# Two graph layers on one core: block sums of the last batch made earlier, the last graph's tail in another order

## The chip, the cores and the metric

One core of a Trainium2 chip. The metric is the device time of one launch in microseconds (us). A profile covers one execution; times without a profile come from further executions on the same chip. Runs e1 to e8 were made on one chip, e9 and e10 on another, each set beside its own nine runs of the kernel before. Medians are given with their number of runs. All timed runs of this study were in the fast state; the runs that were looked at once are of state "unknown", as for any single run on fewer than eight cores, and their mean granted clock (0.996 to 0.998) is that of the fast runs.

## The reference, cut to what matters

64 graphs of 256 nodes with 256 channels go through two layers. The first makes messages between nodes, a convolution along the nodes and the gates of a recurrent cell; the second aggregates over the adjacency. After each layer the result is added to its input and normed.

```python
# layer 0, per graph (n = 256 nodes, d = 256)
x_in = concatenate([x_conv, x_nmp])              # convolution, messages
gi, gh = x_in @ w_ih.T + b_ih, x @ w_hh.T + b_hh
r, z = sigmoid(gi_r + gh_r), sigmoid(gi_z + gh_z)
x = layernorm(x + (1 - z) * tanh(gi_n + r * gh_n) + z * x)
# layer 1
h = layer_norm(x)
agg = einsum('bij,bjh->bih', adj, h)
x = layernorm(x + relu(agg @ W_rel + b_rel + h @ W_root))
```

## The kernel before

The convolution is done for eight graphs (a batch) at a time. It is spread over the graphs of the batch ahead of it: `pump()` lets it go on a little after each piece of a graph. In the traces of this case each engine's operations stand in the order in which the program issues them (VectorE's gn at 2241.99 stayed behind an h that waited for GpSimd, although its input was ready at 2240.24), so the order of the calls below is read as the order on every engine.

The last batch (graphs 56 to 63) has no convolution to hide, and its graphs 56 to 62 compute the gates by a block scheme with seven products in the place of eight. These need sums of blocks of the three inputs (xT, the graph's nodes transposed; nmp, the messages; xc, the convolution), which VectorE makes. Code is cut here and below; `...` marks what is left out:

```python
    def block_sums(k, i):                 # i: 0 = xT, 1 = nmp, 2 = xc
        ...
        nc.vector.tensor_add(s1, a21, a22)
        nc.vector.tensor_sub(s2, s1, a11)
        nc.vector.tensor_sub(s3, a11, a21)
        nc.vector.tensor_sub(s4, a12, s2)
        LEFT[k, i] = (a11, a12, s4, a22, s1, s2, s3)

    def block_gates(k):
        ...
        a, d = bank("ps_a"), bank("ps_d")          # no sums needed
        onto(0, 0, product(a, 0, True), 0)
        onto(0, 0, product(d, 1, True))
        yield
        b_, c_ = bank("ps_b"), bank("ps_c")        # sums of all three inputs
        onto(1, 1, product(b_, 4, True), 1)
        onto(1, 1, product(c_, 6, True))
        yield
        ...

    # between the batches
        for _ in coming:
            pass
    ...
    first_k = (NB - 1) * BG               # graph 56
    for i in range(3):
        block_sums(first_k, i)
    for k in range(first_k, B - 1):
        ...                               # block_gates(k), update(k), second layer of k - 1
    last_graph(y_left, B - 1)
```

The last graph (63) is computed in two halves of 128 nodes, so that its chain (gates, norm, transposes, projection, aggregation, norm, store) can overlap with itself:

```python
        def half(n):
            ...                                    # nn: two operations on VectorE, then
            nc.scalar.activation(a, a, AF.Tanh)
            yield
            ...                                    # w: three operations, statistics on VectorE
            q = scales(mv, [...])                  # root, on GpSimd
            nc.vector.tensor_scalar(H[k][:, n, :], c, mv[:, 0:1], q[:, 1:2], ALU.subtract, ALU.mult)
            sh = shift(mv, q)                      # two GpSimd instructions
            yield
            nc.scalar.activation(X1[k][:, n, :], c, AF.Identity, bias=sh, scale=q[:, 0:1])
            yield
        ...
        gates_n(k, 1)
        step(halves_[1])
        turn_half(0)
        project(k - 1)
        project_half(0)
        step(halves_[1])
        turn_half(1)
        agg = aggregate(k - 1)
        step(agg)
        project_half(1)
        ...
```

Of the kernel before, what the change touches and what calls it, by code (L numbers as in the profile page):

```python
# [29 lines left out]
BG = 8  # L30
# [46 lines left out]
def gnn_two_layers(  # L77
# [357 lines left out]
    def conv(b):  # L435
# [122 lines left out]
        def third(j):  # L558
            stt(sl(V + j, 2, 8), sl(V + j, 2, 8), sv[j], sl(U + j, 2, 8))
            yield cost(2)  # L560
# [25 lines left out]
            yield from second(j)  # L586
        for j in range(8):
            yield from third(j)

        def channels(q):  # L590
            for o in range(C):
# [165 lines left out]
    def block_sums(k, i):  # L757

        if i == 2:
            xc, g = XC[k]  # L760
            v = xc[:, :, g, :]
        else:
            v = (XT, NMP)[i][k]
        a11, a12, a21, a22 = (v[:, c, n * P:(n + 1) * P] for n in range(C) for c in range(C))
        at = S * D + ((k % 2) * 3 + i) * 4 * P
        s1, s2, s3, s4 = (XF[:, at + j * P:at + (j + 1) * P] for j in range(4))
# [5 lines that stand above are left out]
# [102 lines left out]
    def project(k):  # L874
        hT = H[k]
        hr = work.tile([P, C, D], F32, tag="hr", name="hr", bufs=1)
        outs = []
        for n in range(C):
            ps = bank("ps_out")
            for c in range(C):  # L880
                nc.tensor.matmul(ps, hT[:, c, n * P:(n + 1) * P], wrr[:, c, :], start=(c == 0), stop=(c == C - 1))  # L881
            nc.scalar.copy(hr[:, n, :], ps[:, :D])  # L882
            outs.append(ps)
        OUTS[k] = (hr, outs)
# [29 lines left out]
    def step(g):  # L914
        if g is not None:
            next(g, None)


    def last_graph(y_before, k):
        nn, w, y = (work.tile([P, C, D], F32, tag=t, name=t, bufs=b) for t, b in (("nn", 1), ("w", 1), ("y", 2)))  # L920
        H[k] = work.tile([P, C, D], F32, tag="h", name="h", bufs=1)
        X1[k] = work.tile([P, C, D], F32, tag="x1", name="x1", bufs=2)

        hT, hr = (XF[:, i * C * D:(i + 1) * C * D].rearrange("p (c n) -> p c n", c=C) for i in range(2))
        outs = []

        def scales(mv, columns):

            q = work.tile([P, 2], F32, tag="q", name="qh", bufs=4)
            for i, (f, e) in enumerate(columns):  # L930
                nc.gpsimd.tensor_scalar(q[:, i:i + 1], mv[:, 1:2], f, e, ALU.mult, ALU.add)
            nc.gpsimd.tensor_tensor(q[:, :len(columns)], q[:, :len(columns)], mhalf[:, :len(columns)], ALU.pow)
            return q

        def shift(mv, q):
            sh = work.tile([P, 1], F32, tag="sh", name="shh", bufs=4)
            nc.gpsimd.tensor_mul(sh, mv[:, 0:1], q[:, 0:1])
            nc.gpsimd.tensor_scalar(sh, sh, -1.0, None, ALU.mult)
            return sh

        def half(n):
            rz, gn = RZ[k]
            a, c = nn[:, n, :], w[:, n, :]
            stt(a, rz[:, n, :D], 1.0, gn[:, n, D:], op0=ALU.add, op1=ALU.mult)
            stt(a, a, 0.5, gn[:, n, :D])
            nc.scalar.activation(a, a, AF.Tanh)
            yield
            nc.vector.tensor_sub(c, XG[k][:, n, :], a)
            stt(c, rz[:, n, D:], 3.0, c, op0=ALU.add, op1=ALU.mult)
            stt(c, a, 4.0, c)  # L950
            mv = work.tile([P, 1, 2], F32, tag="mv", name="mvh", bufs=4)
            stats(mv, 0, c)
            mv = mv[:, 0, :]
            q = scales(mv, [(1.0, 4 * EPS), (1 + EPS, 4 * EPS * EPS)])
            nc.vector.tensor_scalar(H[k][:, n, :], c, mv[:, 0:1], q[:, 1:2], ALU.subtract, ALU.mult)
            sh = shift(mv, q)
            yield
            nc.scalar.activation(X1[k][:, n, :], c, AF.Identity, bias=sh, scale=q[:, 0:1])
            yield

        def turn_half(n):
            ps = bank("ps_hT")
            for c in range(C):
                nc.tensor.transpose(ps[:, c * P:(c + 1) * P], H[k][:, n, c * P:(c + 1) * P], ident)
            for c in range(C):
                nc.scalar.activation(hT[:, c, n * P:(n + 1) * P], ps[:, c * P:(c + 1) * P], AF.Identity,
                                     bias=gb[:, 1, c:c + 1], scale=gb[:, 0, c:c + 1])

        def project_half(n):
            ps = bank("ps_out")  # L970
            for c in range(C):
                nc.tensor.matmul(ps, hT[:, c, n * P:(n + 1) * P], wrr[:, c, :], start=(c == 0), stop=(c == C - 1))
            nc.scalar.copy(hr[:, n, :], ps[:, :D])
            outs.append(ps)

        halves_ = [half(n) for n in range(C)]
        gates_rz(k, 0)
        gates_n(k, 0)
        step(y_before)
        transposes_h(k - 1)  # L980
        step(halves_[0])
        gates_rz(k, 1)
        step(halves_[0])
        step(halves_[0])
        gates_n(k, 1)
        step(halves_[1])
        turn_half(0)
        project(k - 1)
        project_half(0)
        step(halves_[1])  # L990
        turn_half(1)
        agg = aggregate(k - 1)
        step(agg)
        project_half(1)
        step(halves_[1])
        step(agg)
        for m in range(C):
            for n in range(C):
                nc.tensor.matmul(outs[n][:, D:], ADJ[k][:, m, n * P:(n + 1) * P], hr[:, m, :], start=False,
                                 stop=(m == C - 1), skip_group_check=True)  # L1000
        step(agg)
        for n in range(C):
            o = y[:, n, :]
            nc.vector.tensor_add(o, outs[n][:, D:], brel)
            stt(o, o, 0.0, X1[k][:, n, :], op0=ALU.max, op1=ALU.add)
            mv = work.tile([P, 1, 2], F32, tag="mv3", name="mvy", bufs=4)
            stats(mv, 0, o)
            q = scales(mv[:, 0, :], [(1.0, EPS / 4)])
            sh = shift(mv[:, 0, :], q)
            nc.scalar.activation(o, o, AF.Identity, bias=sh, scale=q[:, 0:1])  # L1010
            (nc.sync, nc.scalar)[n].dma_start(out=out[k, n * P:(n + 1) * P, :], in_=o)


# [108 lines left out]
    POINTS = 10  # L1122
    y_left = None
    sums_left = weight_blocks()
    for b in range(NB):
        coming = conv(b + 1) if b + 1 < NB else iter(())
        done, at, goal = 0.0, 0, BG * POINTS - 6

        def pump():
            nonlocal done, at  # L1130
            at += 1
            while done < CONV_WEIGHT * at / goal:
                t = next(coming, 1e9)
                if t is None:
                    break
                done += t
            if STAGE.get(NB - 1) == "inverse":
                next(sums_left, None)

        if b == NB - 1:  # L1140
            break
        for k in range(b * BG, min((b + 1) * BG, B - 1)):
            load(k + 3)
            load_x(k + 1)
            up = update(k)
            agg = None
            gates_rz(k, 0)
            pump()
            gates_n(k, 0)
            step(y_left)  # L1150
            pump()
            if k > 0:
                transposes_h(k - 1)
            pump()
            gates_rz(k, 1)
            pump()
            if k + 1 < B:
                passing(k + 1)
            pump()
            if k + 2 < B:  # L1160
                factors(k + 2)
            gates_n(k, 1)
            pump()
            if k > 0:
                project(k - 1)
            step(up)
            pump()
            if k + 2 < B:
                distances(k + 2)
            step(up)  # L1170
            pump()
            if k + 3 < B:
                messages(k + 3)
            step(up)
            pump()
            if k + 2 < B:
                mask(k + 2)
            if k > 0:
# [3 lines that stand above are left out]
            pump()  # L1182
            y_left = agg
        for _ in coming:
            pass
    for _ in sums_left:
        pass
    first_k = (NB - 1) * BG
    for i in range(3):
        block_sums(first_k, i)  # L1190
    for k in range(first_k, B - 1):
        load(k + 3)
# [74 lines left out]
```

## Time and profile before

| | before |
|---|---|
| median of 3 runs | 2264.42 us (2263.78 to 2267.38) |
| span of the profiled run | 2261.8 us |
| TensorE busy | 2211.9 us (98%) |
| VectorE busy | 1720.1 us (76%) |

The page, the waits and the timelines that matter are shown in the prediction below. To compare many runs, I cut each trace at four points, and use two stretches throughout:

- the **transition**: from the first matmul of graph 56's ps_a to the ps_hT that follows it. Both kernels have the same twelve fp32 matmuls in it, which the trace shows as twenty-four rows (x2 for each);
- the **tail**: from the first matmul of ps_rz of graph 63 to the issue of the last store.

The two starts in the kernel before, from TensorE's timeline. A row has the start and the duration in us, the engine (PE is TensorE, DVE VectorE, ACT ScalarE, POOL GpSimd, ACTq ScalarE's queue of transfers), the line of the program, the operation, what it writes <- what it reads, the shapes and the number of instructions merged; a bracket gives the idle time of the engine just before it and what ended that:

```profile
2054.70 0.59 PE L785 MATMUL ps_a<-whh,xT 128*128 128x256 f32 x2
...
2224.15 1.88 PE L712 MATMUL ps_rz<-whh,xT 128*128 128x512 f32 x4
```

With ps_hT at 2066.78 the transition is 2066.78 - 2054.70 = 12.08 us, and with the last store at 2258.93 the tail is 34.78 us.

### The profile page before, as it was taken

Reading aid. Unit: us, or ns where it says so; the run is one execution under the profiler, and the core shown is the slowest. Engines: PE = TensorE matmul, PEld = TensorE weight load, DVE = VectorE, ACT = ScalarE, POOL = GpSimd, SP = SyncE. Lnnn points to the kernel's source line nnn. Section 1 sums busy time; section 2 is a strip of 40 time slices with the busy share of each in tenths; the row PEclk is TensorE's granted clock in tenths of the full one; section 3 lists DMA queues with packets and bytes.
Section 4 is the critical chain, followed back from the end, with each engine's and each line's share of the span. In section 5 each row is a group of like instructions: output and inputs, shape, how many; then the busy total and the mean of one; then the engine's idle time right before and its main releaser. Section 6 shows DMA issues by size and latency. Waiting matters only on the chain.

```text
span 2261.8 us, 24648 instructions
## 1 busy us (share of the span) xinstructions
PE 2211.9 (98%) x8400; PEld 1463.5 (65%) x8400; DVE 1720.1 (76%) x3328; ACT 767.7 (34%) x1588; POOL 469.9 (21%) x935
## 2 busy tenths in 40 slices
PE   8999999999999999999999999999999999999998
PEld 5775666666665666656666666665666666666664
DVE  6966889388883988749886497956889388896675
ACT  6433223532234322443224432253223432233333
POOL 0101212221220221213112121221212221222122
PEclk9999999999999999999999999999999999999999
DMA  5932433214423153232522243232432314421110
GB/s 148 316 112 65 139 103 98 98 43 140 135 75 103 38 166 104 79 103 79 163 68 83 91 129 127 70 98 67 138 107 90 100 48 140 135 75 38 42 33 19
DMA packets 212682, 226.69 MB, mean 100 GB/s; under 512 B 22103, under 2 KB 203854, under 8 KB 212558
## 3 DMA queue, kind: packets, MB, share of 16 engines
q1 hardware_dynamic: 190128, 191.27, 26.8%
q10 hardware_dynamic: 22430, 33.86, 4.3%
q8 instruction: 67, 1.10, 0.2%
q14 instruction: 57, 0.47, 0.1%
HBM read 179.22 MB, written 45.88 MB: 100 GB/s over the span
## 4 chain that ended last, share of the span: by engine, by line
PE 79%; DVE 16%; issue 2%; POOL 1%; ACT 1%; DMA 1%; ACTq 0%; POOLq 0%; DVEq 0%
PE ps_rz L714 15%; PE ps_k L385 10%; PE ps_rz L712 8%; PE ps_n L726 7%; PE ps_out L881 7%; DVE XF L104 5%; PE ps_c L466 5%; PE ps_nmp L696 5%; PE ps_msg L646 4%; PE ps_out L893 4%; PE ps_n L724 4%; PE ps_w L230 2%; DVE w L104 2%; DVE bst L823 1%; PE ps_xc L594 1%
## 5 line engine op out<-in xcount | busy, mean ns | idle before, releaser
L104 DVE SCALAR_TENSOR_TENSOR XF<-XF 128x512 f32<-128x512 f32 (+2 forms) x800 | 507.3, 664 | 7.4
L845 POOL TENSOR_SCALAR q<-mv 128x2 f32<-128x2 f32 x63 | 31.8, 506 | 1448.8 <-DVE mv L824 1448.8
L385 PE MATMUL ps_k<-w,XF 128*128 128x256 f32 x1316 | 300.6, 384 | 14.7 <-ACT AT L686 11.6
L385 PEld LDWEIGHTS ps_k<-w,XF 128*128 128x128 f32 x1316 | 247.5, 191 | 62.7 <-ACT AT L686 17.2
L727 DVE TENSOR_TENSOR gn<-ps_n,brzn 128x512 f32<-128x512 f32 x114 | 78.1, 685 | 199.9 <-PE ps_n L726 199.9
L718 ACT ACTIVATE rz<-rz 128x512 f32<-128x512 f32 x114 | 71.8, 630 | 461.4 <-DVE rz L717 461.4
L881 PE MATMUL ps_out<-wrr,hT 128*128 128x512 f32 x504 | 226.6, 592 | 0.0
L712 PE MATMUL ps_rz<-whh,xT 128*128 128x512 f32 x456 | 215.5, 595 | 0.0
L714 PE MATMUL ps_rz<-wih,xc 128*128 128x512 f32 x456 | 214.3, 592 | 0.0
L714 PE MATMUL ps_rz<-wih,nmp 128*128 128x512 f32 x456 | 214.3, 592 | 0.0
L717 DVE TENSOR_TENSOR rz<-ps_rz,brzn 128x512 f32<-128x512 f32 x114 | 77.5, 680 | 155.0 <-PE ps_rz L714 155.0
L881 PEld LDWEIGHTS ps_out<-wrr,hT 128*128 128x128 f32 x504 | 95.7, 190 | 96.1 <-issue 84.2
L714 PEld LDWEIGHTS ps_rz<-wih,xc 128*128 128x128 f32 x456 | 86.7, 190 | 109.0 <-issue 108.8
L714 PEld LDWEIGHTS ps_rz<-wih,nmp 128*128 128x128 f32 x456 | 86.7, 190 | 109.0 <-issue 109.0
L657 ACT ACTIVATE msg<-msg 128x512 f32<-128x512 f32 x61 | 38.4, 630 | 338.8 <-DVE msg L655 338.8
L646 PE MATMUL ps_msg<-wms,xT 128*128 128x260 f32 x512 | 131.9, 395 | 4.6 <-DVE XF L401 4.6
L362 DVE TENSOR_TENSOR XF<-XF 128x512 f32<-128x512 f32 (+3 forms) x128 | 126.1, 1010 | 1.7
L466 PE MATMUL ps_c<-xTc,w 128*128 128x512 f32 x256 | 116.1, 596 | 6.9 <-ACT xTc L458 6.9
L696 PE MATMUL ps_nmp<-AT,msg 128*128 128x256 f32 x512 | 121.1, 379 | 0.0
L712 PEld LDWEIGHTS ps_rz<-whh,xT 128*128 128x128 f32 x456 | 82.7, 192 | 58.3 <-issue 55.1
L882 ACT COPY hr<-ps_out 128x256 f32<-128x256 f32 x126 | 46.8, 372 | 214.7 <-PE ps_out L881 214.7
L893 PE MATMUL ps_out<-hr,adj 128*128 128x256 f32 x504 | 119.5, 380 | 0.0
(196 smaller groups left out, 3787.8 us busy)
## 6 DMA issues: line engine op xcount, KB each, us to landing
w<-w2m SPq DMA_DIRECT2D x105, 768.0 KB, 5.9
xn<-in_x_dram SPq DMA_DIRECT2D x32, 512.0 KB, 4.4
xt<-xTc ACTq DMA_DIRECT2D x32, 512.0 KB, 3.3
xT<-xt SPq DMA_DIRECT2D x64, 256.0 KB, 3.0
xb<-in_x_dram SPq DMA_DIRECT2D x32, 512.0 KB, 5.9
adj<-in_adjT_dram SPq DMA_DIRECT2D x64, 256.0 KB, 2.8
x<-in_x_dram SPq DMA_DIRECT2D x64, 256.0 KB, 3.0
out_dram<-y ACTq DMA_DIRECT2D x63, 256.0 KB, 2.2
```

What stands on the lines that cost most here:

```text
L104: nc.vector.scalar_tensor_tensor(o, in0, s, in1, op0=op0, op1=op1)
L362: (nc.vector.tensor_add if add else nc.vector.tensor_sub)(sl(o, n), sl(a, n), sl(b, n))
L385: nc.tensor.matmul(ps, X[:, slot, c * P:(c + 1) * P], w(m, c), start=(c == 0), stop=(c == C - 1))
L466: nc.tensor.matmul(pss[o], w1[:, c, o * P:(o + 1) * P], xTc[:, c, :], start=(c == 0), stop=(c == C - 1))
L646: nc.tensor.matmul(ps[:, :D + 4], XT[k][:, c, m * P:(m + 1) * P], wms[:, c, :], start=(c == 0), stop=(c == C - 1 and not idle))
L696: nc.tensor.matmul(ps[:, d * N:(d + 1) * N], MSG[k][:, m, d * P:(d + 1) * P], AT[k][:, m, :], start=(m == 0), stop=(m == C - 1))
L712: nc.tensor.matmul(prz, XT[k][:, c, q], whh[:, c, 0:2 * D], start=(c == 0), stop=False)
L714: nc.tensor.matmul(prz, t, wih[:, i, 0:2 * D], start=False, stop=(i == 3))
L724: nc.tensor.matmul(pn[:, D:], XT[k][:, c, q], whh[:, c, 2 * D:], start=(c == 0), stop=(c == C - 1))
L726: nc.tensor.matmul(pn[:, :D], t, wih[:, i, 2 * D:], start=(i == 0), stop=(i == 3))
L881: nc.tensor.matmul(ps, hT[:, c, n * P:(n + 1) * P], wrr[:, c, :], start=(c == 0), stop=(c == C - 1))
L893: nc.tensor.matmul(po, ADJ[k][:, m, n * P:(n + 1) * P], hr[:, m, :], start=False, stop=(m == C - 1), skip_group_check=True)
```

## The change

Its intent: take TensorE's wait for the sums away by making them where VectorE idles, in the batch before; let the second half of the last graph start on VectorE before the first half's root is back from GpSimd, with TensorE's order to match; and let VectorE apply the last norm, so that two GpSimd instructions and one of ScalarE fall off the end. In `pump()` one set of sums goes out per call, once the last batch's convolution is in its output stage and graph 56's messages are there; the condition on `done` keeps the last set, that of xc, until that convolution has run out.

```diff
@@ conv(b)
         for j in range(8):
             yield from third(j)
+        STAGE[b] = "out"
@@ half(n)
             q = scales(mv, [(1.0, 4 * EPS), (1 + EPS, 4 * EPS * EPS)])
+            yield
             nc.vector.tensor_scalar(H[k][:, n, :], c, mv[:, 0:1], q[:, 1:2], ALU.subtract, ALU.mult)
@@ last_graph
         step(halves_[0])
-        step(halves_[0])
         gates_n(k, 1)
         step(halves_[1])
+        step(halves_[0])
+        step(halves_[0])
+        project(k - 1)
+        step(halves_[1])
         turn_half(0)
-        project(k - 1)
-        project_half(0)
         step(halves_[1])
-        turn_half(1)
         agg = aggregate(k - 1)
         step(agg)
+        turn_half(1)
+        step(halves_[1])
+        project_half(0)
         project_half(1)
-        step(halves_[1])
         step(agg)
@@ last_graph, last norm
-            sh = shift(mv[:, 0, :], q)
-            nc.scalar.activation(o, o, AF.Identity, bias=sh, scale=q[:, 0:1])
+            if n == 0:
+                sh = shift(mv[:, 0, :], q)
+                nc.scalar.activation(o, o, AF.Identity, bias=sh, scale=q[:, 0:1])
+            else:
+                nc.vector.tensor_scalar(o, o, mv[:, 0, 0:1], q[:, 0:1], ALU.subtract, ALU.mult)
@@ main loop
+    early_sums = [0, 1, 2]
@@ pump()
-            if STAGE.get(NB - 1) == "inverse":
+            if STAGE.get(NB - 1) in ("inverse", "out"):
                 next(sums_left, None)
+            if STAGE.get(NB - 1) == "out" and (NB - 1) * BG in NMP and len(early_sums) > (done < 1e8):
+                block_sums((NB - 1) * BG, early_sums.pop(0))
@@ behind the batches
-    for i in range(3):
+    for i in early_sums:
         block_sums(first_k, i)
```

## The prediction

> **What bounds the kernel now.** I read the page first. TensorE is the bound from end to end:
>
> ```profile
> PE 2211.9 (98%) x8400; PEld 1463.5 (65%) x8400; DVE 1720.1 (76%) x3328; ACT 767.7 (34%) x1588; POOL 469.9 (21%) x935
> ```
>
> Of a span of 2261.8 us TensorE is idle for 2261.8 - 2211.9 = 49.9 us, so no change that leaves its work alone can win more than 2.2%. This change adds or removes no matmul. It works on two places only, so the next view is what TensorE waited for in the last 262 us (engine, line, releaser; then total us, times, longest):
>
> ```profile
> PE ps_b L785 <- DVE XF L767: 2.7, 2, 2.5
> PE ps_hT L964 <- DVE h L955: 2.3, 2, 2.0
> ```
>
> The first wait is where the last batch's first graph (56) starts: its blocked products need sums of blocks that VectorE makes. The second is in the last graph. The timeline of TensorE at the first place (start us, us, then the instructions merged), with graph 57 below for comparison:
>
> ```profile
> 2060.83 0.67 PE L785 MATMUL ps_b<-wsum,XF 128*128 128x256 f32 x2 [2.52 <-DVE XF L767]
> 2061.69 2.27 PE L785 MATMUL ps_b<-wsum,XF 128*128 128x384 f32 x4 [0.19 <-DVE XF L767]
> 2063.76 3.19 PE L785 MATMUL ps_c<-wsum,XF 128*128 128x256 f32 x6
> 2066.78 0.60 PE L868 MATMUL ps_hT<-ident,h 128*128 128x128 f32 x4
> ...
> 2087.25 1.89 PE L785 MATMUL ps_b<-wsum,XF 128*128 128x256 f32 x6
> ...
> 2090.69 0.60 PE L868 MATMUL ps_hT<-ident,h 128*128 128x128 f32 x4
> ```
>
> The matmuls ahead of ps_b started at 2057.50 and streamed until 2058.14 (as the same pair in graph 57: 2086.60 to 2087.25). From there to ps_hT graph 56 takes 2066.78 - 2058.14 = 8.64 us, graph 57 takes 2090.69 - 2087.25 = 3.44 us for the same twelve instructions. The excess is 5.20 us: more than the 2.7 us of waits in the list. The windows tell why (columns: stretch, length, busy PE, PEld, DVE, ACT, POOL, then the granted clock, DMA share, GB/s):
>
> ```profile
> 2060.80:2063.70 2.90, 2.66 (x6) 1.22 (x7) 2.83 (x12) 1.09 (x2) 1.40 (x4) 0.87 0.00 0
> 2063.70:2066.70 3.00, 3.00 (x7) 1.80 (x6) 1.09 (x3) 0.00 (x0) 0.00 (x0) 0.55 0.26 87
> ```
>
> After the hole the clock falls to about half for some 3.6 us. Now VectorE's timeline before that hole, to see whether the sums could be made sooner:
>
> ```profile
> 2041.75 0.69 DVE L717 TENSOR_TENSOR rz<-ps_rz,brzn 128x512 f32<-128x512 f32 x1 [3.99 <-PE ps_rz L714]
> 2047.16 0.69 DVE L727 TENSOR_TENSOR gn<-ps_n,brzn 128x512 f32<-128x512 f32 x1 [4.72 <-PE ps_n L726]
> ...
> 2051.53 0.69 DVE L836 TENSOR_TENSOR w<-x,nn 128x512 f32<-128x512 f32 x1 [2.15 <-ACT nn L832]
> ...
> 2060.43 0.26 DVE L767 TENSOR_TENSOR XF<-xT 128x128 f32<-128x128 f32 x1
> ```
>
> The bracket is the idle time ahead of a row. VectorE stood idle for 3.99, 4.72 and 2.15 us, and made the sums only at 2060.43, last in its queue. Finally the tail, all engines:
>
> ```profile
> 2241.67 0.41 DVE L955 TENSOR_SCALAR h<-w,mvh,qh 128x256 f32<-128x256 f32 x1 [1.36 <-POOL qh L932]
> ...
> 2241.99 0.68 DVE L727 TENSOR_TENSOR gn<-ps_n,brzn 128x512 f32<-128x512 f32 x1
> ...
> 2242.23 0.41 PE L964 MATMUL ps_hT<-ident,h 128*128 128x128 f32 x2 [1.99 <-DVE h L955]
> ...
> 2247.54 0.41 DVE L955 TENSOR_SCALAR h<-w,mvh,qh 128x256 f32<-128x256 f32 x1 [1.37 <-POOL qh L932]
> ...
> 2257.10 0.58 POOL L932 TENSOR_TENSOR qh<-qh,mhalf 128x1 f32<-128x1 f32 x1
> 2257.38 0.36 SPq L1011 DMA_DIRECT2D out_dram<-y  x1
> ...
> 2258.30 0.60 ACT L1010 ACTIVATE y<-y,shh,qh 128x256 f32<-128x256 f32 x1 [0.94 <-POOL shh L938]
> 2258.93 0.35 ACTq L1011 DMA_DIRECT2D out_dram<-y  x1
> ```
>
> VectorE's queue is in order: h of the first half waits 1.36 us for GpSimd's root, and gn of the second half stands behind it although its PSUM was ready at 2240.24. The end hangs on that second half: gn 2241.99, h 2247.54, then matmuls, two norms, and the store issued at 2258.93.
>
> [...] the trace's sums took 0.26 to 0.30 us, and 2.78 us for all twelve from start to start (2060.43 to 2063.21). [...] I use the starts of what follows a GpSimd instruction.
>
> **Part 1, the block sums.** The built order of VectorE shows twelve additions moved: the four of xT go behind the second rz of graph 55, the four of nmp behind its gn, the four of xc behind its two nn. Nothing is added. Costs: 4 x 0.23 = 0.93 us each. The xT sums fall into 4.72 us of idle (2042.4 to 2047.16): free. The nmp sums (copy of nmp done at 2046.4, in time) push nn from 2047.96 to about 2048.8, its end to about 2050.3; ScalarE's tanh of nn stands behind the copy of hr that starts at 2050.60 anyway, so nothing is later. The xc sums take 2050.3 to 2051.2, ahead of w at 2051.53: free.
> TensorE then runs on: ps_b at 2058.14, ps_c at 2059.86, ps_hT at 2061.58. What might bind next: h for ps_hT (done 2057.30), and VectorE's read of ps_a, which now follows the statistics of y at 2060.43 and ends at about 2061.0, against 2062.0 where TensorE needs it. So the whole 8.64 - 3.44 = 5.20 us goes: about 2.9 us of waiting for sums, the rest the slow clock and smaller waits behind it. From 2067 to 2209 TensorE has no gap in this trace, so the gain is carried to the end: -5.2 us.
>
> **Part 2, the order of the last graph.** h of the first half moves behind nn of the second. Then gn starts when ps_n is there and the statistics are done, about 2240.32 instead of 2241.99. From gn to h of the second half the old trace has 2247.54 - 2241.99 = 5.55 us; the first h (0.41) drops into the 0.48 us that VectorE waits for tanh there, cost about 0.05. So h starts at 2240.32 + 5.55 + 0.05 = 2245.92, 1.62 sooner. TensorE meanwhile does project of graph 62 (2240.08 to 2243.52), one pair of transposes and the aggregation to about 2245.5, then idles about 1 us for h. Behind h, old and new have 0.24 us of transposes and then 3.44 us of matmul before the last aggregation (old: adjacency and half a projection; new: two half projections), and the hr copy bounds the last aggregation alike. So the aggregation and all behind it come 1.62 us sooner, even though project_half(0) now stands behind the idle time.
>
> **Part 3, last norm on VectorE.** Old: from the end of the root (2257.69) two GpSimd instructions and ScalarE, DMA issued at 2258.93: 1.24 us. New: one VectorE operation of 0.41 us, like h, which starts 0.03 us behind the root (2241.64 to 2241.67), and 0.07 us to the queue: 0.51. Gain 0.73 us. The two stores of 128 KB now start 0.82 instead of 1.55 us apart and may share the engines: +0.1.
> Sum, all estimates from these rows: -5.2 - 1.62 - 0.73 + 0.1 = -7.4 us; 2264.42 - 7.4 = 2257.0 us, 0.33%.
>
> **Rivals.** (a) The moved sums delay graph 55: if idle time were not there, up to 2.8 us would come back in w and its norm. For: nmp does push nn by 0.9. Against: the three idle times above. It would leave 2259.8. (b) The clock drop is not the hole's doing[...] and only the waits go: 2.9 instead of 5.2, time 2259.3. Against: the granted clock reads 1.00 in every stretch I sampled around it. (c) In the tail the idle 1 us before the second transposes, or the projection placed behind it, eats the 1.62: then 2258.6; and if the clock dropped there, about 2 us more. Against: the old tail's hole of 1.99 us left the clock at 1.00. (d) TensorE binds on VectorE's read of ps_a sooner than I put it: up to 0.9 us, as before graph 62's ps_a at 2209.97.
>
> **Range and chances.** The three runs of before spread over 3.6 us, half of the effect, so the range is the rivals (up to +2.5) and that spread: 2254.5 to 2260.5. The verdict line of 2% is 45 us away; TensorE's idle time altogether is 50 us, and slower by 45 us would need a loss in a part that is not touched. Within 2%: 0.98, faster 0.01, slower 0.01.
>
> **What would show it.** Right: no wait of ps_b for the sums; graph 56's ps_b to ps_hT in 3.4 us at clock 1.00; ps_hT of graph 55 near 2061.6; the second h of the tail about 5.6 us behind its gn and 6.8 us sooner in absolute time; no GpSimd shift before the last store, whose issue lies about 7.5 us sooner, at 2251.4; span near 2254.3. Wrong: nn, w or y of graph 55 later than before, a clock below 0.9 anywhere behind 2055, a hole before the second transposes above 1.5 us, or last rows that are sooner by less than 5 us.

## The result, and the profile after

| | before | changed | ratio of fast runs, 95% interval |
|---|---|---|---|
| first timing | 2265.89 us (4 runs) | 2255.80 us (4 runs, 2254.62 to 2256.83) | 0.9956 [0.9939, 0.9973] |
| timed again | 2261.97 us (9 runs, 2259.09 to 2265.19) | 2254.73 us (5 runs, 2252.30 to 2256.18) | 0.9968 [0.9956, 0.9981] |

A ratio is the mean time of one kernel's fast runs over that of the other's fast runs of the same rounds, so it is not quite the ratio of the medians. Both timings are "same" by the 2% rule, and both are clearly faster. The first says 10 us and the second 7.2; the prediction said 7.4. What is known of the difference stands under e9.

The profiled run of the changed kernel has a span of 2252.8 us, 9.0 less. TensorE's waits from 2000 us on (total, times, longest) no longer name the sums, and the wait for h in the tail is down from 1.99 at its longest to 0.6:

```profile
PE ps_a L786 <- DVE XF L791: 0.9, 1, 0.9
PE ps_dist L685 <- ACT lr L676: 0.7, 1, 0.7
PE ps_hT L966 <- DVE h L957: 0.6, 1, 0.6
```

TensorE's timeline of the transition, and the start of the tail:

```profile
2053.25 0.60 PE L786 MATMUL ps_a<-whh,xT 128*128 128x256 f32 x2
...
2056.69 1.89 PE L786 MATMUL ps_b<-wsum,XF 128*128 128x256 f32 x6
2058.41 1.89 PE L786 MATMUL ps_c<-wsum,XF 128*128 128x256 f32 x6
2060.13 0.60 PE L869 MATMUL ps_hT<-ident,h 128*128 128x128 f32 x4
...
2217.52 1.88 PE L713 MATMUL ps_rz<-whh,xT 128*128 128x512 f32 x4
```

No bracket, so no idle time: ps_b to ps_hT takes 3.44 us where it took 5.95 from ps_b's late start and 8.64 from the end of ps_d. The transition is 6.88 us, 5.20 less. The granted clock in that stretch (columns as in the prediction: stretch, length, busy times of five engines, clock, DMA share, GB/s) is full, where it had been 0.55 and 0.87:

```profile
2056.70:2060.20 3.50, 3.50 (x14) 2.29 (x13) 3.26 (x10) 0.10 (x1) 2.00 (x5) 1.00 0.00 0
```

VectorE's timeline shows where the sums went. The last row's bracket is the idle time that is left ahead of w, which has not moved against TensorE (w is 3.18 us ahead of ps_a's first matmul, as it was 3.17 before):

```profile
2040.90 0.28 DVE L768 TENSOR_TENSOR XF<-xT 128x128 f32<-128x128 f32 x1
...
2046.32 0.28 DVE L768 TENSOR_TENSOR XF<-nmp 128x128 f32<-128x128 f32 x1
...
2048.57 0.29 DVE L768 TENSOR_TENSOR XF<-xc 128x128 f32<-128x128 f32 x1
...
2050.07 0.69 DVE L837 TENSOR_TENSOR w<-x,nn 128x512 f32<-128x512 f32 x1 [0.49 <-ACT nn L833]
```

The tail, all engines:

```profile
2233.64 0.69 DVE L728 TENSOR_TENSOR gn<-ps_n,brzn 128x512 f32<-128x512 f32 x1
...
2239.19 0.41 DVE L957 TENSOR_SCALAR h<-w,mvh,qh 128x256 f32<-128x256 f32 x1 [1.37 <-POOL qh L933]
...
2239.66 0.44 PE L966 MATMUL ps_hT<-ident,h 128*128 128x128 f32 x2 [0.61 <-DVE h L957]
...
2247.14 0.85 POOL L933 TENSOR_TENSOR qh<-qh,mhalf 128x1 f32<-128x1 f32 x1
...
2248.65 0.19 POOL L932 TENSOR_SCALAR qh<-mvy 128x1 f32<-128x1 f32 x1
2248.92 0.58 POOL L933 TENSOR_TENSOR qh<-qh,mhalf 128x1 f32<-128x1 f32 x1
...
2249.54 0.41 DVE L1017 TENSOR_SCALAR y<-y,mvy,qh 128x256 f32<-128x256 f32 x1 [1.29 <-POOL qh L933]
2249.98 0.35 ACTq L1018 DMA_DIRECT2D out_dram<-y  x1
```

From gn to the second h it is 5.55 us, as before; gn itself comes sooner. The tail is 2249.98 - 2217.52 = 32.46 us, 2.31 less. One thing is new: VectorE's statistics of the second half are done at 2248.24, but the second root begins at 2248.65, because GpSimd is still busy with the first half.

So the profile's 9.0 us are 5.20 in the transition, 2.31 in the tail, and 1.45 ahead of graph 56 (its ps_a starts at 2053.25 instead of 2054.70), where the two programs are the same until the sums at 2040.90. That last part lies within the scatter of this stretch, which the next section shows.

### The profile page after: what moved, and what is told of

It reads as the page before. It is cut to its first block, busy times and chain, and to the rows that moved or that the text cites. A ratio compares the mean times of both kernels' runs of the same rounds, so it can differ in the third digit from the quotient of the medians.

```text
span 2252.8 us, 24641 instructions
## 1 busy us (share of the span) xinstructions
PE 2210.0 (98%) x8400; PEld 1465.9 (65%) x8400; DVE 1721.0 (76%) x3329; ACT 767.1 (34%) x1587; POOL 469.8 (21%) x933
## 4 chain that ended last, share of the span: by engine, by line
PE 80%; DVE 15%; issue 2%; POOL 1%; ACT 1%; DMA 1%; ACTq 0%; SPq 0%; POOLq 0%; DVEq 0%
PE ps_rz L715 15%; PE ps_k L385 11%; PE ps_rz L713 8%; PE ps_n L727 7%; PE ps_out L882 7%; PE ps_c L466 5%; DVE XF L104 5%; PE ps_nmp L697 5%; PE ps_msg L647 4%; PE ps_out L894 4%; PE ps_n L725 4%; PE ps_w L230 2%; DVE w L104 2%; DVE bst L824 1%; PE ps_dist L685 1%
```

## The experiments

Every run gave a correct result. The table has the cuts of each trace: what lies ahead of graph 56's ps_a, the transition, from there to the tail, the tail, and from the last store's issue to the end of the span (us). It is made from unrounded times, so it can differ by 0.01 from a difference of two rows shown.

| run | ahead | transition | middle | tail | end | span |
|---|---|---|---|---|---|---|
| before | 2054.70 | 12.08 | 157.37 | 34.77 | 2.83 | 2261.8 |
| changed | 2053.25 | 6.89 | 157.38 | 32.46 | 2.83 | 2252.8 |
| e1, sums alone | 2056.76 | 6.89 | 157.37 | 35.95 | 2.82 | 2259.8 |
| e2, tail alone | 2052.63 | 12.01 | 157.37 | 32.47 | 2.82 | 2257.3 |
| e3, two of three sums early | 2050.75 | 8.52 | 157.38 | 32.46 | 2.83 | 2251.9 |
| e4, hole filled | 2054.65 | 10.40 | 157.38 | 34.77 | 2.83 | 2260.0 |
| e5, last norm on ScalarE | 2054.49 | 6.89 | 157.37 | 33.25 | 2.82 | 2254.8 |
| e6, VectorE's order alone | 2054.95 | 6.89 | 157.37 | 33.70 | 2.83 | 2255.7 |
| e7, TensorE's order alone | 2056.99 | 6.89 | 157.38 | 34.20 | 2.82 | 2258.3 |
| e8, both last norms on VectorE | 2060.27 | 6.89 | 157.38 | 32.20 | 2.82 | 2259.6 |
| e9, changed kernel again | 2053.39 | 6.89 | 157.37 | 32.48 | 2.82 | 2252.9 |
| e10, split projection | 2055.73 | 6.89 | 157.37 | 31.40 | 2.83 | 2254.2 |

Read the columns first. The middle, 157 us, is the same to 0.01 us in twelve runs. "Ahead", which no experiment touched but for the place of twelve small VectorE additions in its last 13 us, scatters from 2050.75 to 2060.27; with the sums late (before, e2, e4) it is 2052.63 to 2054.70, inside the range of the others. So a whole time cannot resolve 2 us from a few runs, while a cut of a trace resolves 0.1.

### e1: the sums alone

```diff
 # from the kernel before
+        STAGE[b] = "out"
...
+            if STAGE.get(NB - 1) == "out" and (NB - 1) * BG in NMP and len(early_sums) > (done < 1e8):
+                block_sums((NB - 1) * BG, early_sums.pop(0))
...
-    for i in range(3):
+    for i in early_sums:
```

> The kernel before with the early block sums alone. Two stretches are read in every run: the transition (start of graph 56's first ps_a matmul to the start of the following ps_hT; 12.08 us before, 6.88 us after) and the tail (start of the last graph's first ps_rz matmul to the issue of the last store; 34.78 before, 32.46 after). Theory: transition 6.9, tail 34.8, time 5.2 us under before (ratio 0.9977). Rival (only the waits of 2.9 us go, the slow clock stays): transition 9.2, time 2.9 us under. Rival (the parts need each other): transition above 7.5.

Measured: transition 6.89 as the theory has it; 2258.61 us (5 runs) against 2264.39 (9 runs), ratio 0.9981 [0.9968, 0.9993], which holds the 0.9977 expected and leaves out the 2.9 us rival only by the transition, not by the time. The tail missed: 35.95 instead of 34.8. The tail's instructions are those of before. This run's timeline of TensorE, and the clock of the stretch:

```profile
2239.33 5.30 PE L882 MATMUL ps_out<-wrr,hT 128*128 128x512 f32 x8
```

```profile
2240.00:2243.00 3.00, 3.00 (x5) 1.25 (x4) 2.35 (x7) 1.17 (x4) 0.00 (x0) 0.54 0.00 0
```

The eight rows of project took 5.30 us; in the profile before they took 3.60. Ahead of them stands the same hole of 1.99 us in both, but here the clock fell to half behind it (0.54, where the profile before has 1.00 from 2242.2 to 2245). I had used this hole in the prediction, under rival (c), as a sign that 2 us are harmless. They are not always. By the estimate under e8, the window of 3.41 us that ended where the drop began was 36% full of matmul work in this run; in the profile before, the emptiest window at this hole was 47% full.

### e2: the tail alone

```diff
 # from the changed kernel: the sums at their old place
-        STAGE[b] = "out"
...
-            if STAGE.get(NB - 1) == "out" and (NB - 1) * BG in NMP and len(early_sums) > (done < 1e8):
-                block_sums((NB - 1) * BG, early_sums.pop(0))
...
-    for i in early_sums:
+    for i in range(3):
 # half(), last_graph and the last norm stay as changed
```

> The kernel before with the new order of the last graph and its last norm on VectorE, the block sums late. Theory: transition 12.1 with the clock falling to about half behind the hole, tail 32.5, time 2.3 us under before (ratio 0.9990), less than the scatter of single runs. Rival (the tail gain needs the earlier sums): tail 34 or more.

Measured: transition 12.01 and tail 32.47, both as expected; the tail's gain does not need the sums. The clock was 0.51 for 3.4 us behind the hole. In the time, 2262.47 us (5 runs, 2259.09 to 2267.22) against 2264.39, the ratio is 0.9999 [0.9986, 1.0013]: the expected 0.9990 lies in it, and so does nothing at all. By time alone this run is inconclusive.

### e3: two of three sums early

```diff
-            if STAGE.get(NB - 1) == "out" and ... and len(early_sums) > (done < 1e8):
+            if STAGE.get(NB - 1) == "out" and ... and len(early_sums) > 1:
```

> The changed kernel, but the four sums of xc stay behind the statistics of y; those of xT and nmp are early. ps_b then has 1.07 us of matmul before it needs a late sum, so the hole is about 1.6 us instead of 2.7. Theory (a hole this short leaves the clock alone, so the loss is the wait only): ps_hT some 1.6 us later than in the changed kernel, transition 8.5. Rival (any pause here drops the clock): transition about 10, granted clock about half behind it.

Measured: transition 8.52. TensorE waits once, for the sums of xc, and the clock stays up:

```profile
2056.80 0.91 PE L786 MATMUL ps_b<-wsum,XF 128*128 128x384 f32 x2 [1.36 <-DVE XF L768]
```

```profile
2056.00:2059.00 3.00, 2.20 (x8) 1.49 (x9) 2.83 (x10) 0.70 (x2) 1.37 (x4) 1.00 0.00 0
```

A late xc alone costs 8.52 - 6.89 = 1.63 us, with no slow clock in it. The third set of sums is worth as much as it takes to wait for, and no more, when the clock holds. That it held behind 1.36 us is one run's, and e8 has a drop behind a wait of 1.12 us; by the estimate under e8 it was not luck here, since the emptiest window of 3.41 us that can be laid over this hole is 56% full.

### e4: the hole filled

```diff
         onto(0, 0, product(d, 1, True))
+        if k == (NB - 1) * BG:
+            fill = bank("ps_fill")
+            for _ in range(12):
+                nc.tensor.matmul(fill[:, :P], ones, ones, start=True, stop=True)
         yield
```

> The kernel before, with twelve idle matmuls (ones by ones, 128 columns, result unread) behind graph 56's ps_d, about 2.6 us of work in the place of the hole; the sums stay late. Theory (the hole lets the clock fall): granted clock 1.00 through ps_b and ps_c, ps_c back to 1.7 us, the waits for the sums stay; transition about 10.3. Rival (the slow stretch comes from VectorE or from a clock that falls on its own): ps_c still near 3 us, transition about 12.

Measured: transition 10.40, against 10.3 expected and 12 of the rival. ps_c is back to its usual time although nothing but useless work was added, and the clock of the stretch that had 0.55 is full:

```profile
2063.32 1.89 PE L785 MATMUL ps_c<-wsum,XF 128*128 128x256 f32 x6
```

```profile
2063.70:2066.70 3.00, 3.00 (x15) 2.08 (x14) 1.60 (x4) 1.01 (x2) 0.00 (x0) 1.00 0.26 87
```

This separates the two causes: of the 5.20 us, 12.08 - 10.40 = 1.68 were the slow clock that the hole brought, and the remaining 3.51 the waits for the sums (ps_b starts 6.13 us behind ps_a with and without the filling). One run alone could owe its full clock to chance: of the two holes of 1.99 us, one had a drop behind it (0.54, e1) and the other had none (1.00, before). The estimate under e8 speaks against that. In e4's own windows of 3.41 us the one that ends in ps_b is 86% full; without the filling's rows it would be 27% full, and the drops came behind windows of 41% (before) and 32% (e2). So I put the drop here down to the idle time: the clock was 0.55 behind it, and 1.00 where it was filled.

### e5: the last norm on ScalarE again

```diff
-            if n == 0:
+            if True:
                 sh = shift(mv[:, 0, :], q)
```

> The changed kernel with the second half's last norm back on GpSimd and ScalarE; early sums and new order kept. Theory: the tail is longer by the 0.75 us that two GpSimd instructions and ScalarE take more than VectorE, so about 33.2 us against 32.46; the reordering alone is then 34.77 - 33.2 = 1.6. Rival (GpSimd is busy with the first half's shift either way, and the norm's engine hardly matters): tail 32.6.

Measured: tail 33.25. The norm's move is worth 33.25 - 32.46 = 0.79 us, the reordering 34.77 - 33.25 = 1.52. The rival is out.

### e6 and e7: one engine's order alone

```diff
 # e6, from the changed kernel: TensorE's calls as before
         step(halves_[0])
+        turn_half(0)
         project(k - 1)
+        project_half(0)
         step(halves_[1])
-        turn_half(0)
         step(halves_[1])
+        turn_half(1)
         agg = aggregate(k - 1)
         step(agg)
-        turn_half(1)
-        step(halves_[1])
-        project_half(0)
         project_half(1)
+        step(halves_[1])
```

> The changed kernel with VectorE's new order in the last graph (h of the first half behind nn of the second) but TensorE's old order. Theory: the second h comes 1.6 us sooner, but TensorE now waits for the first h (about 2.3 us) and then has 5.2 us of projections ahead of the second transposes, which so come no sooner than before; tail about 34.1 (only the norm's 0.5 and 0.1 to 0.2 are left), more if the hole drops the clock. Rival (VectorE's order is the whole gain): tail 32.5.

```diff
 # e7, from the changed kernel: the first half's h ahead of the second half's gn, as before
-        gates_n(k, 1)
-        step(halves_[1])
         step(halves_[0])
         step(halves_[0])
+        gates_n(k, 1)
+        step(halves_[1])
```

> The changed kernel with TensorE's new order but VectorE's old one (first h ahead of gn of the second half). Theory: the second h comes where it came before, 23.4 us behind the tail's start, the hole ahead of its transposes grows to about 2.6 us, nothing is won but the norm: tail about 34.2[...]. Rival (TensorE's order is the whole gain): tail 32.5.

Measured: tails 33.70 and 34.20, against 34.1 and 34.2 expected. TensorE's wait for h in e6 and in e7:

```profile
PE ps_hT L966 <- DVE h L957: 2.2, 1, 2.2
```

```profile
PE ps_hT L966 <- DVE h L957: 1.6, 1, 1.6
```

Neither order alone has the 32.46 of both. In e6 the second h is ready early, but TensorE idles 2.2 us for the first h and then still has project and half a projection to do. In e7 TensorE has worked ahead, but the second h comes as late as ever; the wait is 1.6 us, not the 2.6 that I expected; the aggregation also waited 0.5 us for ScalarE's copy of hr and so took a part of the hole, and the rest of the miss was not traced. Whichever engine is mended alone, the other becomes the bound. In e6 I was 0.4 us too high: there the last norm gives its full 0.76 and not the 0.5 that I had put in, as GpSimd does not run late, and the second transposes come 0.28 us sooner than before, where I had expected no gain.

### e8: both last norms on VectorE

```diff
+        roots = []
         for n in range(C):
...
-            q = scales(mv[:, 0, :], [(1.0, EPS / 4)])
-            if n == 0:
-                sh = shift(mv[:, 0, :], q)
-                nc.scalar.activation(o, o, AF.Identity, bias=sh, scale=q[:, 0:1])
-            else:
-                nc.vector.tensor_scalar(o, o, mv[:, 0, 0:1], q[:, 0:1], ALU.subtract, ALU.mult)
+            roots.append((mv, scales(mv[:, 0, :], [(1.0, EPS / 4)])))
+        for n, (mv, q) in enumerate(roots):
+            o = y[:, n, :]
+            nc.vector.tensor_scalar(o, o, mv[:, 0, 0:1], q[:, 0:1], ALU.subtract, ALU.mult)
             (nc.sync, nc.scalar)[n].dma_start(out=out[k, n * P:(n + 1) * P, :], in_=o)
```

> The changed kernel with the last norm of both halves on VectorE, behind both statistics, so that GpSimd makes the two roots with no shift between. Theory (in the changed kernel the second root waits about 0.3 us for the first half's shift on GpSimd): second root straight behind its statistics, tail about 32.1. Rival (the root itself sets it): tail 32.46 as in the changed kernel.

Measured: tail 32.20, 0.26 less, against 0.36 expected and none by the rival. The second root no longer stands behind the shift: it begins 0.09 us behind its statistics (done at 2255.27), as in the kernel before, instead of 0.41.

```profile
2255.09 0.18 DVE L825 BATCH_NORM_AGGREGATE mvy<-bst 128x2 f32<-128x6 f32 x1
...
2255.36 0.26 POOL L932 TENSOR_SCALAR qh<-mvy 128x1 f32<-128x1 f32 x1 [0.34 <-DVE mvy L825]
```

Of the 0.32 us so won some 0.05 are lost again behind it: from there to the last norm it takes 0.94 us, against 0.89 in the changed kernel; why was not tested.

This run also had the longest stretch "ahead", and a part of the reason is in its trace. At an early graph TensorE waited 1.12 us for ScalarE, and then ran at half clock for 3.4 us:

```profile
290.55 5.62 PE L385 MATMUL ps_k<-w,XF 128*128 128x256 f32 x17 [1.12 <-ACT AT L687]
```

```profile
290.60:294.00 3.40, 3.40 (x8) 2.75 (x9) 3.30 (x7) 0.74 (x2) 0.00 (x0) 0.51 0.00 0
```

The same wait of 1.12 to 1.13 us is there in all the other runs; of these e5 alone dropped at it too. In the clock records of all twelve traces, each drop ahead of the transition lasts 3.41 us, or twice that, and within one trace all drops start whole multiples of 3.41 us apart (before: 830.8 and 2063.0, 1232.2 = 361 x 3.413), with another phase in each run. The runs with the shortest stretch ahead have two of them there (e3, 2050.75), the longest five (e8, 2060.27); at half clock one of 3.41 us costs up to half of that, 1.7 us. That makes up a part of the scatter; the rest was not traced, and e9, also with two, is 2.6 us longer there than e3.

What stands ahead of a drop can be read from these records. I cut each trace into windows of 3.41 us at the places where its own drops start, and count how much of each window is full of matmul work: each row at the start-to-start time of its shape in a full-clock stream (0.43 us for 512 columns, 0.32 for 384, 0.22 for 256, 0.11 for 128; twice that in a drop), the products of ps_dist, which use 4 of 128 rows, as nothing. This is an estimate, made when the drops were known. Ahead of 2245 us, all 41 drops of the twelve traces start behind a window that is at most 41% full; of the 7765 windows without a drop behind them, six are under 41% full and none is under 39%. The length of one gap does not decide it alone: the clock fell to half behind a wait of 1.12 us (e8) and a hole of 1.99 us (e1), and held behind the same hole of 1.99 us in the kernel before and behind 1.36 us in e3. By the estimate it goes with how little work falls into one window (41% at most), and the windows, cut at the drops, lie differently in each of the twelve traces. No run was built to test this.

### e9: the changed kernel again

```diff
 # no edit
```

> The changed kernel unaltered, timed again, because single runs of one kernel scatter by some 6 us. Theory (segments of the traces: 5.2 in the transition, 2.3 in the tail, nothing elsewhere): ratio 0.9967, an interval that holds it, and medians 7.5 us apart. Rival (the 10 us of the first timing are real and a part of the gain lies ahead of the change): ratio 0.9956 again, and the stretch ahead of graph 56 shorter than in most other runs (below 2052 us).

Measured: 2254.73 us against 2261.97, ratio 0.9968 [0.9956, 0.9981]; transition 6.89, tail 32.48. This is the theory's 0.9967. The first timing's 10 us are some 2.6 more than the trace's two stretches; its interval, [0.9939, 0.9973], holds 0.9968 as well, and the stretch ahead was 1.45 us shorter in its profiled run. So I put them down to scatter; what the chip does to it was not separated (e9's is another than that of e1 to e8, and that of the first timing is not on record).

### e10: split projection

```diff
 # e8, and project_half becomes a generator that yields after each matmul
         step(agg)
+        first_half = project_half(0)
+        step(first_half)
         turn_half(1)
         step(halves_[1])
-        project_half(0)
-        project_half(1)
+        for part in (first_half, project_half(1)):
+            for _ in part:
+                pass
```

> The changed kernel with both last norms on VectorE and the first matmul of project_half(0) placed ahead of the second transposes, where TensorE idles 0.6 us. Theory: the hole is filled, one matmul of 0.43 us less stands behind the second h on the way to the last aggregation, transposes start up to 0.3 later; tail about 31.9 against 32.2 of both norms alone and 32.46 of the changed kernel; time 8 us under before. Rival (the second half's projection waits for ScalarE's copy of the transposes): tail 32.2 or more.

Measured: tail 31.40, 1.06 under the changed kernel and 0.5 under what I expected. TensorE's timeline:

```profile
2241.36 1.02 PE L974 MATMUL ps_out<-wrr,XF 128*128 128x512 f32 x2
2242.22 0.41 PE L966 MATMUL ps_hT<-ident,h 128*128 128x128 f32 x2
```

The matmul placed in the hole shows as two rows, 0.86 us from start to start, not the 0.43 that I had put down: the fp32 matmuls of the program are two rows each in the trace (twelve as twenty-four in the transition and in e4's filling). In the time it cannot be told from the changed kernel: 2254.54 us against 2254.73, both at a ratio of 0.9968 to before. The trace says that its tail is the shortest, by 0.80 us against e8 and by 1.06 against the changed kernel; the timing does not resolve that.

## Why the prediction was right

The predicted 2257.0 us holds: 2255.80 and 2254.73 measured, inside 2254.5 to 2260.5, and the 7.4 us of gain came out as 7.5 in the trace's two stretches and as 7.2 in the second timing (0.9968 of 2261.97). The gain is the better test: the kernel before itself measured 2264.42 (3 runs), 2264.39 (9) and, on the other chip, 2261.97 (9), so how close the absolute time came is in part luck.

- **Part 1, 5.2 us.** Measured 5.19. No engine took the wait's place, w of graph 55 stayed where it was, and the 157.4 us behind it passed the gain on unchanged. Its division was less exact: I gave the waits about 2.9 us and the rest to "the slow clock and smaller waits"; e4 shows 1.68 for the clock and 3.51 for the waits.
- **Part 2, 1.62 us.** Measured 1.52 (e5). The second h came 1.71 us sooner in its stretch (6.64 us is the shift of all rows at that point, h moved from 2247.54 to 2239.19, 8.35), and the additions behind the last aggregation 1.79. Then some 0.3 us went back on GpSimd: the first half's root took 0.85 us instead of 0.57 (what follows it on GpSimd starts 0.93 us behind its start, against 0.64 before), and the second half's root, behind it in the same queue, began 0.41 us behind its statistics instead of 0.09. In all eight traces with the long root, VectorE's operation on y and x starts within 0.003 us of it; in the four with the short one it starts 0.07 us behind it. Whether that lengthens the root was not tested. I had looked for queues on VectorE and TensorE and not on GpSimd.
- **Part 3, 0.73 us.** Measured 0.79 (e5). The 0.1 us set aside for two stores that might share the engines, a guess that no row of the trace showed, did not come: from the last issue to the end it is 2.83 us in both.
- **The absolute times** that I named for the changed trace were late by 1.4 us (last store at 2249.98, not 2251.4), since I took the stretch ahead as fixed. It is the one that scatters most.
- **Rivals.** (a), sums that delay graph 55, is out by the trace of the changed kernel. (b) had the clock drop for another reason than the hole; the drops of a trace do start whole multiples of 3.41 us apart (e8), but with the hole filled the clock was 1.00 where it had been 0.55 (e4). My argument against (b) was right but thin. (c), a new hole in the tail, was there (0.61 us) and did not eat the gain, but it was not free either: with a matmul put into it, e10's tail is 0.80 us shorter than e8's. The reason I gave for the clock, that the old hole of 1.99 us had left it alone, fell with e1. (d) did not show.
- **A reading that does not stand as written.** The 49.9 us of idle time are called a limit of what can be won; yet of the 5.20 us only 2.7 were idle time, and 2.5 came out of rows counted as busy, as those at half clock are.

## What to carry to other kernels

When the bounding engine waits for small work of another engine, look in that engine's timeline for idle time that lies between the sources' readiness and the use, and issue the work there: twelve additions moved into idle time gave 5.2 us at no cost that the cuts show. Count the clock with the wait: waits of 2.7 us had a clock of 0.55 behind them, which cost 1.68 us more; with the hole filled by useless matmuls the clock was 1.00 and only the wait was left (e4). In a tail made of one chain over four engines, both sides of a hand-over have to be reordered together (here 33.70 and 34.20 us with one engine's order alone, 32.46 with both), and gains of 1 to 2 us are read from cuts of the trace, not from a time that scatters by 6 us (2259.09 to 2265.19 in nine runs of the kernel before).
